# A four-stage transformer kernel on one core: another order of work at its beginning, between its stages and at its end

## The chip, the cores and the metric

The kernel runs on one core of a Trainium2 chip. A core has several engines that run side by side, each through its own queue in order: PE (TensorE) multiplies matrices and transposes, DVE (VectorE) and ACT (ScalarE) work on tiles element by element, POOL (GpSimd) also does so (a product of 128 x 512 takes it 1.26 us here, DVE 0.69) and issues the indirect DMAs, and SP (SyncE) issues the other DMAs. PE writes its products to PSUM, a small memory kept here in banks of 128 x 512 fp32 numbers; DVE, ACT and POOL bring them to SBUF. The engines wait for each other with semaphores. The metric is the device time of one execution in microseconds (us); the median of three runs is given with the lowest and the highest.

## What is computed

Sixteen sequences x of 256 tokens and 256 features, in fp32, go through four stages, each of which adds its gated result to x:

```python
x = x + tanh(g_xattn[0]) * L0_xattn(ctx, layernorm(x))   # stage 0
x = x + tanh(g_ffn[0])   * L0_ffn(layernorm(x))          # stage 1
x = x + tanh(g_xattn[1]) * L1_xattn(layernorm(x), ctx, ctx, fside, mask)   # stage 2
x = x + tanh(g_ffn[1])   * L1_ffn(layernorm(x))          # stage 3
```

- Stage 0 is attention with 16 heads of 64. The 256 queries of a sequence come from the layernorm of its normed rows; keys and values come from those rows and from 77 context rows, so 333 keys in all.
- Stage 1 is a mixture of 8 experts, each a 256 x 256 product; each token takes the two with the highest router probability. Out of the layernorm, `out = sum over the two of (x W_e + prob_e) * weight_e`.
- Stage 2 is attention with 16 heads of 16 over the 77 context rows, with a key mask; the softmax is multiplied by `fside` before the values.
- Stage 3 is gated linear attention with 8 heads of 64 in chunks of 64 tokens. A dense and a routed path are added (the routed one goes to the most probable of 4 experts for each token); then

```python
o = o * rsqrt(mean(o * o, axis=-1) + eps) * norm_w   # over the 64 values of a head
o = o * (g * sigmoid(g))
return o.reshape(B, L, 512) @ Wo
```

A layernorm is `(x - mean) / sqrt(var + 1e-5)` over the 256 features.

## The kernel before

All of x stays in SBUF: `xs[b]` holds sequence b as 128 partitions x 2 x 256. The four stages run one after the other, `stage0_fast` to `stage3_fast`, with parts of each woven into the one before. Beside the result the kernel gathers ten check values (`check`, among them `esum`, the sums of exponentials of stage 0, and `logs`, the logarithms of stage 3's mean squares). `verdict` reduces them to one flag, `bad`; SP loads it, and only if it is set does an exact, slower program run after. It does not run in the profiled execution.

Nearly all operations are put out through `dve`, `act`, `pool` and `pe` (`Pinned`), which keep each engine's instructions in the order in which the program is written. All of these carry line L50 in the profile, so the tile names tell them apart; the products and transposes of stage 3 carry L1523 and L1526. A call of a product is two instructions in the profile, since it is fp32. So the order of the work is written out by hand, by the order of the calls.

**Norms.** `moments` takes mean and variance on DVE (`bn_stats`, then `bn_aggr`, tile `mv`), then POOL adds eps and raises to the power -0.5 (tile `rs`, two small operations). `normed` lets DVE make the bias and ACT scale x, in two halves. Stage 0 norms x (`norm_x`, `normed_y`) and then the normed rows again (`norm_y`, `normed_all`), and the context rows (`norm_c`). `Prepare` (`prep`) does it for stage 2: `stats`, `norm`, `turn` (transposes, an ACT copy) and `queries`.

**Stage 0** loops over 64 units (sequence b, four heads g). `turn` makes kvT, the transposed normed rows, `all_values` the values `v`, `heads` queries and keys of two heads (PSUM to SBUF by ACT and DVE, tile `qk`), `scores` the 24 matmul instructions `sc` in three groups and three exponentials `e` on ACT. `sums` adds the three key chunks on POOL into `es`, and adds those to `esum`. `values` multiplies: `den` by ones with `es`, then e with v (48 instructions, in chunks), and DVE takes the reciprocal and the product `oT`. `project` multiplies by the output weights. A unit's values run one unit behind its scores. `heads` of the next unit is called behind the values. Stage 1's routing is called from tables (`ahead_of`, `behind_scores`, `behind_values`): its weighted rows `xw` are scattered by POOL's indirect DMAs into `rows`, sorted by expert. Before the loop stand the calls for batch 0, then the norms of batch 1, then `heads(0, 0, 0)` and `heads(0, 0, 1)`.

**Stage 1** has 48 units in two halves of 24 (eight sequences each): the rows of one expert (`xin`, fetched by SP at L1051) are transposed (`xT`, copied by ACT), multiplied (`ex`), copied by DVE (`y`) and stored by SP (L1076, `rows_out`). In the second half POOL gathers results back into x by indirect DMA (`next_gather`, 64 in all), and a table, `steps`, calls stage 2's `prep.stats` for b = 0, 1, 2.

**Stage 2** loops over b = 0 to 16; b does the scores of sequence b in two halves c (`sc`, one PSUM buffer of four banks, then one exponential of 77 x 2048 on ACT), weighs them by `fside` on DVE (`pg`), multiplies by the values, and projects sequence b-1. `prep` runs two and three sequences ahead: `prep.stats(b + 3)` stands at the end of the loop's body. In the last rounds `early` calls `next` on stage 3's generator, whose first groups (norm of sequence 0, transposes, gates, routing) so run between stage 2's parts; a letter says at which b.

**Stage 3** then loops over p = 0 to 66 for 64 positions (sequence b, pair of heads m): `keys_queries` (kq), `decays` (gq, gz), `second`, `factors` (f, q), `products` (sc), `masked` (tile `at`: DVE multiplies the dense half by a mask and, for the routed half, by `kden` and a mask; POOL adds the two), and one position later `values` (o). Every second position, `squares`, `gated` (u) and `scaled` (mean square `ms`, Ln and Exp on ACT, and POOL's product `oT`), and for each sequence `project` (16 matmul instructions, one addition on DVE, one DMA of 256 KB, L1813). PSUM tiles of its own pool `psu` have one bank each (kq, gq, gz, o). The last three rounds do only what is left of position 63, and `verdict` (L1907) stands ahead of the last `project`.

Of the kernel before, what the change touches and what calls it, by code (L numbers as in the profile page):

```python
# [17 lines left out]
P = 128  # L18
B, S, D = 16, 256, 256
S2 = 77  # L20
EPS = 1e-5
# [52 lines left out]
def layers(ctx: ExitStack, tc: tile.TileContext, t, out, check):  # L74
# [79 lines left out]
    nc.gpsimd.memset(ones, 1.0)  # L154
    gate = const("gate", [P, 4])
# [26 lines left out]
    def moments(src, p=P, n=2):  # L182
# [5 lines left out]
        for i in range(n):  # L188
            dve.bn_aggr(mv[:p, i, :], bst[:p, i, :])
        pool.tensor_scalar(rs[:p, 0, :n], mv[:p, :n, 1], 1.0, EPS, ALU.mult, ALU.add)  # L190
# [336 lines left out]
    def stage0_fast():  # L527
        with ExitStack() as sx:
# [106 lines left out]
            def values(b, g, e, es):  # L635
# [6 lines left out]
                for h, r in heads:  # L642
                    n, j = divmod(h, 2)
                    pe.matmul(den[r, :S], ones[:KC, :32], es[:, n, j * S:(j + 1) * S], start=True, stop=True)
# [39 lines left out]

            norm_c(0)
            norm_x(0)
            normed_y(0)
            norm_y(0)
            normed_all(0)
            turn(0)  # L690
            all_values(0)
            norm_c(1)
# [3 lines left out]
            heads(0, 0, 0)  # L696
            heads(0, 0, 1)
# [34 lines left out]
            values(*behind)  # L732
# [402 lines left out]
    class Prepare:  # L1135
# [12 lines left out]
        def stats(self, b):  # L1148
            self.mv[b] = moments(xs[b])
# [29 lines left out]
    def stage2_fast(prep, bank, begin):  # L1179
        with ExitStack() as sx:  # L1180
# [71 lines left out]
            for b in range(B + 1):  # L1252
# [22 lines left out]
                run(project, b - 1)  # L1275
                route.next_gather()
# [3 lines left out]
                early(a=1, b=1, c=1, d=1)  # L1280
# [224 lines left out]
    def stage3_fast(early_bank):  # L1505

        with ExitStack() as sx:
# [22 lines left out]
            eps = w1.tile([P, 1], F32, tag="eps", name="eps")  # L1530
            pool3.memset(eps, EPS)
# [219 lines left out]
            def masked(p, n):  # L1751
# [43 lines left out]
            def scaled(b, mp):  # L1795
                ps = bank("ms")
                matmul(ps, halves, sq.pop((b, mp)), start=True, stop=True)
                r = w2.tile([P, 512], F32, tag="r", name="r")
# [3 lines left out]
                pool3.tensor_tensor(oT[b][:, 2 * mp:2 * mp + 2, :].rearrange("p m s -> p (m s)"),  # L1802
                                        u_[b][:, 2 * mp:2 * mp + 2, :].rearrange("p m s -> p (m s)"), r, ALU.mult)

            def project(b):
# [7 lines left out]
                nc.sync.dma_start(out=out[b].rearrange("(c p) d -> p c d", p=P), in_=xs[b])  # L1813

# [183 lines left out]
```

## Time and profile before

| what | value |
|---|---|
| median of 3 runs | 1952.68 us (1947.13, 1952.68, 1958.38) |
| the profiled execution's own time | 1950.77 us |
| its span, first to last instruction | 1949.0 us |
| mean granted PE clock | 0.992 of full |
| busy | PE 1901.1, DVE 1088.5, POOL 1001.3, ACT 869.4 us |
| stage 0 to 1 / 1 to 2 / 2 to 3 in the span | about 980 / 1104 / 1289 us |

The page gives busy time, a row of digits per engine (40 slices of the span, in tenths), the granted PE clock in the same slices, DMA, and the groups of instructions. Behind it stands the trace, which can be asked for waits (an engine, the tile it was to write, and what ended the idle time before), for a timeline (start, duration, engine, tile written and tiles read, how many instructions are put together; in brackets the idle time before it and what ended that), and for windows (length, busy time and number of instructions of PE, PEld, DVE, ACT and POOL, then the granted clock, the DMA share and GB/s). PEld is PE's loading of weights, which runs beside its products. Starts are us from the beginning of the span.

### The profile page before, as it was taken

Reading aid. Unit: us, or ns where it says so; the run is one execution under the profiler, and the core shown is the slowest. Engines: PE = TensorE matmul, PEld = TensorE weight load, DVE = VectorE, ACT = ScalarE, POOL = GpSimd, SP = SyncE. Lnnn points to the kernel's source line nnn. Section 1 sums busy time; section 2 is a strip of 40 time slices with the busy share of each in tenths; the row PEclk is TensorE's granted clock in tenths of the full one; section 3 lists DMA queues with packets and bytes.
Section 4 is the critical chain, followed back from the end, with each engine's and each line's share of the span. In section 5 each row is a group of like instructions: output and inputs, shape, how many; then the busy total and the mean of one; then the engine's idle time right before and its main releaser. Section 6 shows DMA issues by size and latency. Waiting matters only on the chain. (4 is left out here: it accounts for less than half of the span.)

```text
span 1949.0 us, 34915 instructions
## 1 busy us (share of the span) xinstructions
PE 1901.1 (98%) x13986; PEld 1321.0 (68%) x13986; DVE 1088.5 (56%) x2635; ACT 869.4 (45%) x1795; POOL 1001.3 (51%) x905
## 2 busy tenths in 40 slices
PE   7999999999999999999999899999999999999997
PEld 4666676666766666666677666567777777777775
DVE  3334555455545545553464388875666656666564
ACT  3433344434434344343333488744444444444442
POOL 4644757556665557565614756124444444444443
PEclk9999999999999999999999999999999999999998
DMA  9300000000000000000078733000000000000000
GB/s 343 129 1 3 14 11 14 11 9 11 14 11 11 9 11 12 9 12 9 14 250 236 191 49 47 8 1 6 7 6 7 12 7 6 7 6 12 6 7 13
DMA packets 54012, 75.03 MB, mean 38 GB/s; under 512 B 10081, under 2 KB 43729, under 8 KB 53329
## 3 DMA queue, kind: packets, MB, share of 16 engines
q1 hardware_dynamic: 41552, 55.92, 8.5%
q0 software_dynamic: 12288, 16.79, 4.3%
q8 instruction: 112, 1.84, 0.4%
q14 instruction: 60, 0.48, 0.1%
HBM read 39.14 MB, written 33.55 MB: 37 GB/s over the span
## 5 line engine op out<-in xcount | busy, mean ns | idle before, releaser
L50 POOL TENSOR_SCALAR rs<-mv 128x2 f32<-128x2 f32 (+1 forms) x96 | 18.4, 192 | 468.3 <-DVE mv L50 464.4
L50 ACT ACTIVATE qk<-qk 128x256 f32<-128x256 f32 x128 | 49.2, 385 | 339.7 <-PE qk L50 339.7
L50 ACT ACTIVATE e<-sc 111x1024 f32<-111x1024 f32 x192 | 182.3, 1022 | 17.7 <-PE sc L50 17.7
L50 PE MATMUL sc<-qk 64*111 64x256 f32 x1536 | 182.2, 383 | 2.1 <-DVE qk L50 2.1
L50 PE MATMUL o<-e,v 111*32 111x256 f32 x3072 | 179.2, 382 | 0.0
L50 DVE RECIPROCAL rd<-o 128x256 f32<-128x256 f32 x64 | 112.3, 1755 | 103.0 <-PE o L50 103.0
L50 PE MATMUL v<-wkv,kvT 128*111 128x512 f32 x384 | 169.2, 597 | 0.6 <-DVE kvT L50 0.6
L50 PEld LDWEIGHTS sc<-qk 64*111 64x111 f32 x1536 | 132.1, 172 | 55.1 <-issue 28.5
L50 POOL TENSOR_TENSOR esum<-esum,es 111x512 f32<-111x512 f32 x128 | 163.1, 1274 | 10.0
L50 POOL TENSOR_TENSOR es<-e 111x1024 f32<-111x1024 f32 x64 | 151.3, 2364 | 26.5 <-ACT e L50 25.2
L50 PE MATMUL qk<-kvT,wkv 128*128 128x333 f32 x512 | 164.3, 443 | 0.0
L50 POOL TENSOR_TENSOR k<-e,ee 128x256 f32<-128x256 f32 x64 | 47.4, 740 | 222.6 <-ACT e L50 222.6
L50 POOL TENSOR_TENSOR es<-es,e 111x1024 f32<-111x1024 f32 x64 | 150.4, 2349 | 5.0
L50 PEld LDWEIGHTS o<-e,v 111*32 111x32 f32 x3072 | 100.5, 111 | 66.9 <-issue 1.7
L50 DVE COPY qk<-qk 128x333 f32<-128x333 f32 x128 | 64.5, 505 | 126.3 <-ACT qk L50 124.8
L50 PE MATMUL qk<-kvT,wq 128*128 128x256 f32 x512 | 134.3, 385 | 0.0
L50 PEld LDWEIGHTS v<-wkv,kvT 128*111 128x111 f32 x384 | 67.1, 178 | 91.6 <-issue 90.1
L50 POOL TENSOR_TENSOR at<-at,at 128x768 f32<-128x768 f32 x64 | 115.9, 1810 | 25.1 <-DVE at L50 16.0
L50 DVE TENSOR_TENSOR at<-sc,amask 128x768 f32<-128x768 f32 x64 | 61.3, 958 | 116.2 <-PE sc L1523 100.4
L50 POOL DMA_INDIRECT x<-rows_out,pos x64 | 100.4, 1568 | 35.0 <-DMA we<-in_we_dram 16.4
L50 PEld LDWEIGHTS qk<-kvT,wkv 128*128 128x128 f32 x512 | 97.2, 190 | 30.0
L50 PEld LDWEIGHTS qk<-kvT,wq 128*128 128x128 f32 x512 | 94.3, 189 | 34.0 <-issue 13.2
(230 smaller groups left out, 4125.3 us busy)
## 6 DMA issues: line engine op xcount, KB each, us to landing
rows<-zero SPq DMA_DIRECT2D x16, 640.0 KB
xin<-rows SPq DMA_DIRECT2D x16, 640.0 KB
rows_out<-y SPq DMA_DIRECT2D x16, 384.0 KB
x<-in_x_dram SPq DMA_DIRECT2D x16, 256.0 KB
rows_out<-y SPq DMA_DIRECT2D x16, 256.0 KB
out_dram<-x SPq DMA_DIRECT2D x16, 256.0 KB
wkv<-in_wkv_dram SPq DMA_DIRECT2D x2, 1024.0 KB
ew<-in_ew_dram SPq DMA_DIRECT2D x2, 1024.0 KB
```

Of the source, the lines that this page charges most:

```text
L50: x = getattr(self.engine, name)(*a, **k)
```

## The change

1. **Norms by ScalarE.** The constant `eps` is made at the program's start, on POOL, and no more at stage 3's. `moments(by_act=True)` takes Ln(var + eps) and Exp(-0.5 ...) on ACT for the two operations on POOL. It is so for the second norm of batch 0 in stage 0 and for `prep.stats` of b < 5 (three in stage 1, and those at b = 0 and 1 of stage 2).
2. **Beginning.** Products of `ones` with rows of x (four) and with the normed rows (three), into a bank that is not read, stand before the first transposes; `heads(0, 0, 0)` and `heads(0, 0, 1)` stand before the norms of batch 1.
3. **Stage 0 to 1.** In the last `values`, `den` is made from e in three chunks (12 calls for 4) and not from POOL's `es`; `es` and `esum` are still made.
4. **Stage 2 to 3.** The generator's group (norm, turn) is two groups; at b = 14 one `next` more stands after `project(13)`, and that at the end of the body at b = 16 is gone. The last three groups and the opening of `psu` become one step, which begins with `keys_queries(0)` (before, that followed them all).
5. **End.** The loop ends at p = 63. Position 63's dense and routed parts are not added on POOL; `values` multiplies them one after the other into one bank. The last `project` is in four parts (token half i, heads' half h) in the banks of kq and gq, the first ones before the last heads are there; the last scaling is on DVE, two products of `ones` into an unread bank stand beside it, and the output goes by two DMAs of 128 KB. The checks' reductions stand in three parts between these, and the flag is made after the last projection.

```diff
     nc.gpsimd.memset(ones, 1.0)
+    eps = const("eps", [P, 1])
+    nc.gpsimd.memset(eps, EPS)
     gate = const("gate", [P, 4])
...
-    def moments(src, p=P, n=2):
+    def moments(src, p=P, n=2, by_act=False):
         mv = st.tile([P, 2, 2], F32, tag="mv", name="mv")
...
             dve.bn_aggr(mv[:p, i, :], bst[:p, i, :])
+        if by_act:
+            act.activation(rs[:p, 0, :n], mv[:p, :n, 1], AF.Ln, bias=eps[:p])
+            act.activation(rs[:p, 0, :n], rs[:p, 0, :n], AF.Exp, scale=-0.5)
+            return mv, rs
         pool.tensor_scalar(rs[:p, 0, :n], mv[:p, :n, 1], 1.0, EPS, ALU.mult, ALU.add)
...
         return mv, rs
...
-            def values(b, g, e, es):
+            def values(b, g, e, es, last=False):
...
                 heads = [(h, slice(32 * h, 32 * h + 32)) for h in range(4)]
-                for h, r in heads:
-                    n, j = divmod(h, 2)
-                    pe.matmul(den[r, :S], ones[:KC, :32], es[:, n, j * S:(j + 1) * S], start=True, stop=True)
+                for c in range(3 if last else 1):
+                    for h, r in heads:
+                        n, j = divmod(h, 2)
+                        x = e[:, 3 * n + c, j, :] if last else es[:, n, j * S:(j + 1) * S]
+                        pe.matmul(den[r, :S], ones[:KC, :32], x, start=c == 0, stop=not last or c == 2)
                 for i in range(2):
...
                         for h, r in heads:
...
+            def warm(src, n):
+                ps = bank("warm")
+                for _ in range(n):
+                    pe.matmul(ps[:, :D], ones, src, start=True, stop=True)
             norm_c(0)
             norm_x(0)
+            warm(xs[0][:, 0, :], 4)
             normed_y(0)
-            norm_y(0)
+            mvs[0, "y"] = moments(y[0], by_act=True)
+            warm(y[0][:, 1, :], 3)
             normed_all(0)
...
             all_values(0)
+            heads(0, 0, 0)
+            heads(0, 0, 1)
             norm_c(1)
...
             units = [(b, g) for b in range(B) for g in range(4)]
-            heads(0, 0, 0)
-            heads(0, 0, 1)
             behind = None
...
                 ahead = units[n + 1] if n + 1 < len(units) else None
...
             run(behind_scores, B, 0)
-            values(*behind)
+            values(*behind, last=True)
             tally()
...
             run(behind_scores, B, 1)
...
         def stats(self, b):
-            self.mv[b] = moments(xs[b])
+            self.mv[b] = moments(xs[b], by_act=b < 5)
...
                 run(project, b - 1)
+                early(b=1)
                 route.next_gather()
...
                 run(prep.stats, b + 3)
-                early(a=1, b=1, c=1, d=1)
+                early(a=1, b=1, c=1)
                 route.next_gather()
...
             nc.sync.dma_start(out=halves, in_=t["halves"])
-            eps = w1.tile([P, 1], F32, tag="eps", name="eps")
-            pool3.memset(eps, EPS)
...
                                                            am[b][:, lo:hi], ALU.mult, ALU.mult)
+                    if p == last - 1:
+                        at[p] = a
+                        return
                     pool3.tensor_tensor(at[p], at[p], a, ALU.add)
-            def values(p):
+            def values(p, first=True, end=True):
                 b, m, cols = place(p)
...
                     o[b, m // 2] = psu.tile([P, 512], F32, tag="o", name="o")
-                ps, a = o[b, m // 2], at.pop(p)
+                ps, a = o[b, m // 2], at[p] if not end else at.pop(p)
                 base = m % 2 * S
...
                         matmul(ps[64 * j:64 * j + 64, to:base + S], v[b][:, i, h], a[:, j, lo:hi],
-                                         start=i == 0, stop=i == 1)
+                                         start=first and i == 0, stop=end and i == 1)
...
-            def scaled(b, mp):
+            def scaled(b, mp, by=pool3, beside=()):
                 ps = bank("ms")
                 matmul(ps, halves, sq.pop((b, mp)), start=True, stop=True)
+                for x in beside:
+                    x()
                 r = w2.tile([P, 512], F32, tag="r", name="r")
...
                 act3.activation(r, r, AF.Exp, scale=-0.5)
-                pool3.tensor_tensor(oT[b][:, 2 * mp:2 * mp + 2, :].rearrange("p m s -> p (m s)"),
+                by.tensor_tensor(oT[b][:, 2 * mp:2 * mp + 2, :].rearrange("p m s -> p (m s)"),
                                         u_[b][:, 2 * mp:2 * mp + 2, :].rearrange("p m s -> p (m s)"), r, ALU.mult)
             def project(b):
...
+            pp = {}
+            def project_part(b, i, h):
+                if h == 0:
+                    pp[i] = psu.tile([P, 512], F32, tag=("kq", "gq")[i], name=("kq", "gq")[i])
+                for m in (2 * h, 2 * h + 1):
+                    matmul(pp[i][:, :D], oT[b][:, m, tokens(i)], wo[:, m, :], start=m == 0, stop=m == 3)
+                if h == 1:
+                    dve3.scalar_tensor_tensor(xs[b][:, i, :], pp[i][:, :D], gate[:, 3:4], xs[b][:, i, :],
+                                              ALU.mult, ALU.add)
+                    nc.sync.dma_start(out=out[b, tokens(i)], in_=xs[b][:, i, :])
+            def warm():
+                ps = bank("warm")
+                for _ in range(2):
+                    matmul(ps, ones, v[B - 1][:, 0, :], start=True, stop=True)
             start = {0: [(turn, 1)], 2: [(turn_hot, 1)]}
...
             yield
-            for group in (((bias, 0), (stats, 0)), ((norm, 0), (turn, 0)), ((lows, 0),), ((gates, 0, 0),),
+            for group in (((bias, 0), (stats, 0)), ((norm, 0),), ((turn, 0),), ((lows, 0),), ((gates, 0, 0),),
                           ((gate_logs, 0, 0), (route_logits, 0)), ((route_sums, 0), (gates, 0, 1)),
-                          ((route, 0), (vals, 0), (gate_logs, 0, 1), (bias, 1)),
-                          ((turn_hot, 0), (turned_hot, 0), (stats, 1)), ((pairs, 0), (norm, 1)),
-                          ((steepest, 0, 0), (steepest, 0, 1))):
+                          ((route, 0), (vals, 0), (gate_logs, 0, 1), (bias, 1))):
                 for f, *a in group:
...
             psu = sx.enter_context(tc.tile_pool(name="f3psu", bufs=1, space=PSUM, side="right", reuse_waits="tile"))
+            keys_queries(0)
+            for f, *a in ((turn_hot, 0), (turned_hot, 0), (stats, 1), (pairs, 0), (norm, 1), (steepest, 0, 0),
+                          (steepest, 0, 1)):
+                f(*a)
             yield
...
             last = 4 * B
-            keys_queries(0)
             decays(0)
...
             dve3.tensor_scalar(wo, wo3, vec[:, V_NW:V_NW + 1], None, ALU.mult)
-            for p in range(last + 3):
+            for p in range(last):
                 run(start, p)
-                if p < last:
-                    shares(p)
-                if 0 < p <= last:
+                shares(p)
+                if 0 < p:
                     masked(p - 1, 1)
...
-                if p == last + 1:
-                    verdict(bank("verdict"))
-    def verdict(ps):
-        r = st.tile([P, 10], F32, tag="vr", name="vr")
-        bounds = (("esum", E_MOST), ("rsum", R_MOST), ("most", E_MOST), ("uneven", 0.5), ("second", E_MOST),
-                  ("logs", E_MOST), ("gates", G_MOST),
-                  ("rows", ROWS + 0.5), ("rsum2", R_MOST), ("rsum0", R_MOST))
-        for n, (name, bound) in enumerate(bounds):
-            dve.tensor_reduce(r[:, n:n + 1], check[name], AX.XY if name == "rows" else AX.X, ALU.max)
-            dve.tensor_scalar(r[:, n:n + 1], r[:, n:n + 1], bound, None, ALU.is_lt)
-        dve.tensor_reduce(r[:, 0:1], r, AX.X, ALU.min)
-        dve.tensor_scalar(r[:, 0:1], r[:, 0:1], 0.0, None, ALU.is_equal)
-        nc.tensor.matmul(ps[0:1, 0:1], r[:, 0:1], ones[:, 0:1], start=True, stop=True)
-        dve.tensor_copy(check["bad"], ps[0:1, 0:1])
+            b, p = B - 1, last - 1
+            values(p, end=False)
+            masked(p, 1)
+            project_part(b, 0, 0)
+            values(p, first=False)
+            ends = Verdict()
+            ends.part("esum", "most", "uneven", "second", "rows")
+            squares(b, 1)
+            gated(b, 1)
+            ends.part("rsum", "gates", "rsum2", "rsum0")
+            scaled(b, 1, dve3, [lambda: project_part(b, 1, 0), warm])
+            for i in range(2):
+                project_part(b, i, 1)
+            ends.part("logs")
+            ends.end(bank("verdict"))
+    class Verdict:
+        bounds = {"esum": E_MOST, "rsum": R_MOST, "most": E_MOST, "uneven": 0.5, "second": E_MOST, "logs": E_MOST,
+                  "gates": G_MOST, "rows": ROWS + 0.5, "rsum2": R_MOST, "rsum0": R_MOST}
+        def __init__(self):
+            self.r, self.n = st.tile([P, 10], F32, tag="vr", name="vr"), 0
+        def part(self, *names):
+            for name in names:
+                r = self.r[:, self.n:self.n + 1]
+                dve.tensor_reduce(r, check[name], AX.XY if name == "rows" else AX.X, ALU.max)
+                dve.tensor_scalar(r, r, self.bounds[name], None, ALU.is_lt)
+                self.n += 1
+        def end(self, ps):
+            r = self.r
+            assert self.n == len(self.bounds)
+            dve.tensor_reduce(r[:, 0:1], r, AX.X, ALU.min)
+            dve.tensor_scalar(r[:, 0:1], r[:, 0:1], 0.0, None, ALU.is_equal)
+            pe.matmul(ps[0:1, 0:1], r[:, 0:1], ones[:, 0:1], start=True, stop=True)
+            dve.tensor_copy(check["bad"], ps[0:1, 0:1])
...
         with tc.tile_pool(name="ctx_side", bufs=1) as keep, tc.tile_pool(name="f12w2", bufs=2) as keep2:
...
             stage2_fast(prep, shared_bank, last_stage)
-            for _ in range(3):
-                next(last_stage)
+            next(last_stage)
         s_banks.close()
...
             pass
```

More of the change, by code (lines that the diff above doesn't have):

```diff
@@ L1856, in stage3_fast @@
             dve3.tensor_scalar(wo, wo3, vec[:, V_NW:V_NW + 1], None, ALU.mult)
-            for p in range(last + 3):
+            for p in range(last):
                 run(start, p)
-                if p < last:
-                    shares(p)
-                if 0 < p <= last:
+                shares(p)
+                if 0 < p:
                     masked(p - 1, 1)
                 run(copies, p)
-                if 1 < p <= last + 1 and p % 2 == 1:
+                if 1 < p and p % 2 == 1:
                     gated((p - 2) // 4, (p - 2) % 4 // 2)
-                if p < last:
-                    shares_end(p)
+                shares_end(p)
                 if p + 1 < last:
@@ L1874, in stage3_fast @@
                 run(late, p)
-                if p < last:
-                    products(p, 0)
-                    masked(p, 0)
+                products(p, 0)
+                masked(p, 0)
                 run(behind_mask, p)
@@ L1885, in stage3_fast @@
                 run(logs, p)
-                if p < last:
-                    products(p, 1)
-                if 0 < p <= last:
+                products(p, 1)
+                if 0 < p:
                     values(p - 1)
```

## The prediction

> **What bounds the kernel now.** I read the page's busy times first, then the PE and clock digits, the chain of waits of PE, and the timeline at the places that it names.
>
> ```profile
> PE 1901.1 (98%) x13986; PEld 1321.0 (68%) x13986; DVE 1088.5 (56%) x2635; ACT 869.4 (45%) x1795; POOL 1001.3 (51%) x905
> PE   7999999999999999999999899999999999999997
> PEclk9999999999999999999999999999999999999998
> ```
>
> PE works 98% of the span, so time is won only where PE stands, or runs at half clock. The waits of PE, longest first (us in total, times, longest):
>
> ```profile
> PE tr L50 <- ACT xn L50: 10.8, 1, 10.8
> PE ex L50 <- ACT xT L50: 5.0, 4, 2.3
> PE o L50 <- POOL es L50: 3.2, 1, 3.2
> PE o L1523 <- POOL at L50: 3.0, 1, 3.0
> PE verdict L1907 <- DVE vr L50: 3.0, 1, 3.0
> PE tr L1526 <- DVE xn L50: 2.4, 1, 2.4
> ```
>
> They lie at the beginning, at the passages and at the end, where the change is. What a wait costs beyond itself is in the timeline and the windows:
>
> ```profile
> 13.33 12.20 PE L50 MATMUL v<-wkv,kvT 128*111 128x512 f32 x24 [0.64 <-DVE kvT L50]
> 968.09 0.64 PE L50 MATMUL o<-es,ones 111*32 111x256 f32 x8 [3.19 <-POOL es L50]
> 968.55 4.46 PE L50 MATMUL o<-e,v 111*32 111x256 f32 x48
> 13.33:16.70 3.37, 3.37 (x4) 1.37 (x5) 0.93 (x3) 0.00 (x0) 0.00 (x0) 1.00 1.09 351
> 16.70:20.10 3.40, 3.40 (x9) 1.41 (x8) 0.69 (x1) 0.59 (x1) 0.00 (x0) 1.00 1.10 348
> 969.00:972.40 3.40, 3.40 (x40) 1.72 (x36) 0.00 (x0) 0.00 (x0) 2.65 (x3) 0.50 0.00 0
> 1929.03 1.55 PE L1523 MATMUL o<-at,v 128*64 128x256 f32 x8 [3.02 <-POOL at L50]
> 1936.43 6.36 PE L1523 MATMUL proj<-wo,oT 128*128 128x256 f32 x16
> 1942.83 0.75 DVE L50 SCALAR_TENSOR_TENSOR x<-proj,gate,x 128x512 f32<-128x512 f32 x1 [6.14 <-PE proj L1523]
> ```
>
> After the 3.19 us gap the granted clock is 0.50 (the column before the last two) for one stretch of 3.4 us: 48 products take 4.46 us, against 2.77 one unit earlier. The 2.29 us gap at 991.7 and the 1.92 at 1110.8 are followed by 0.5 too. At the start four instructions of `v` run in the first 3.37 us and nine in the next 3.40: half rate, though the clock column reads 1.00. The last projection takes 6.36 us cold; warm, at 1912.96, 3.62.
>
> **The sum**, against the profiled execution's 1950.77 us (span 1949.0); the median of the runs shown is 1952.68 (1947.13 to 1958.38), 1.91 higher.
>
> *Beginning, +1.0 (-2.0 to +2.65).* POOL's two steps (0.19 and 0.69 us) with their hand-overs, 8.85 to 9.85, become two small ACT operations of some 0.2 (rows with 128x2 elements on ACT are 0.17 to 0.21): 0.5 saved. The 14 added matmul instructions go into PE's first 10.76 us, idle now, so they cost nothing; if they came late, the transposes would queue behind them, 14 x 0.2 at most. They may raise the clock before `v`. Its first 3.4 us at half rate lose 1.7, and the transposes lose 0.45. With the 0.5 that is 2.65. Against it: with heads(0,0) moved past the norms of batch 1, DVE's statistics for c and x, POOL's powers and ACT's y(1), hidden before under the head products, come after the copies of qk. The exps stand in ACT's order behind y(1) (1.09): 34.45 less the gain, where they began at 32.81, and sc(0,1) comes at 39.75 less the gain, where it was at 38.59: 1.15 lost, 1.5 left. PE then stands 1.3 and 2.35 in 5.5 us, and such gaps halve the clock for a stretch (1.7) in some places and not in others: half of it is 0.85. I take 1.0, between 1.5 and 0.65. The lower end is without warm products (2.15 less) and with the whole stretch (0.85 less). The eps memset (0.69 on POOL at 1107.94, for which nobody waits) goes to POOL's idle start: nothing; before the first rs it has 2.09 us of cover, and beyond that would delay the start by 0.69.
>
> *Stage 0 to 1, +4.0 (+2.3 to +4.0).* den reads e directly: 24 instructions for 8, 16 x 2.77/48 = 0.92 more. e is there since 962.34, so the 3.19 goes, and the half clock behind it (4.46-2.77 = 1.7): 3.19+1.7-0.92 = 4.0. POOL's es and esum stay, for the checks, beside PE. Next late is xin's transfer: on SP it waits for PE's values and for POOL's esum (968.12+2.63 = 970.75), so its issue moves from 973.20 to 970.9 only, 2.3 earlier. Had it only just landed at 980.03, where xT reads it without a wait, the gain would be 2.3. But three loads of 640 KB are under way until 981.6, and xT needs the first: I take 4.0. The scatters that POOL issues next wait for landings as before and stand ahead of no product.
>
> *Stage 1's second half, +1.7 (0 to +2.1).* POOL full of gathers (1.54 each) gives rs at 1078.3 for statistics that were done at 1070.54, and ex waits 2.14 at 1080.18 for ACT's xT behind xn. By ACT, rs is there at 1071. Each Ln holds ACT for DVE's statistics: 0.45 over the three places, in which ACT's xT copies are queued and PE waits for them.
>
> *Stage 2, b=0 and 1, -3.0 (0 to -6.0).* No wait is taken away here, and one is added. ACT's Ln stands before the next exp and waits for bn_aggr: at 1118.2 where the exp started at 1116.94 (delay 1.7), and 1130.25 where it started at 1128.07:
>
> ```profile
> 1127.94 0.66 PE L50 MATMUL tr<-ident,xn 128*128 128x128 f32 x4
> 1128.07 1.96 ACT L50 ACTIVATE e<-sc,neg 77x2048 f32<-77x2048 f32 x1
> 1129.91 0.30 DVE L50 BATCH_NORM_AGGREGATE mv<-bst 128x2 f32<-128x6 f32 x2
> ```
>
> With two ops of 0.2 the second exp is 2.6 late. The sc at 1130.39 has one PSUM buffer and needs that exp's end (1130.03, then 1132.6): PE stands 2.2. At b=0 the sc at 1120.35 needs 1118.9+1.7 = 1120.6: 0.25. Behind the waiting Ln stand the exp, gpx's and xnT's copies; DVE's pg and PE's q wait for those. 2.45 in all, and 0.55 for the chance (a third) that the gap halves the clock. Both delays in full (4.3) and a whole stretch (1.7) make 6.0; if the later waits of this stage absorb them, 0. POOL, relieved of two powers here, had slack.
>
> *Stage 2 to 3, +1.0 (+0.3 to +1.7).* project(13), ready at 1254.66, now fills the 2.45 us in which turn(0) waits for xn at 1256.26: +1.73. keys_queries(0) ahead of turn_hot(0) puts eight matmul instructions (1.13 and 1.03 overlapping, 1.84) before hT; hT's copy then no longer stands 0.39 behind the addition on DVE, so DVE's chain (em, am, xn, steepest, f) is 1.45 later: f ended at 1288.18, now 1289.63, and kq(1), which has one bank and came at 1288.91, waits for it: -0.74. If the chain is not later, +1.7; if it is later by all of 1.45, +0.3.
>
> *End, +8.2 (+7.6 to +8.7).* values(63) no longer waits for POOL's add (1927.17, 1.80): its two halves, with project's first part between, end at 1928.5 instead of 1930.58. sq .60, ms warm 1.12 and Ln, accumulator, Exp .69+.19+.63 bring r at 1931.7 (before 1934.9); DVE multiplies in .69 instead of POOL's 1.26; eight matmul instructions remain, 1.8 warm, and an addition of .43: 1934.98 instead of 1943.58, 8.6 earlier. Two warm products (four instructions of .5) lie in the 1.5 us wait for r, behind project's part; if they ran cold, 4 us, they would delay the last part. The two stores of 128 KB need one more SP issue (.37), the first 0.9 early. The checks' reduces (.68 for esum, .41 for rsum, the rest .15 to .2) stand between on DVE and are done before r. The verdict, finished ahead of the projection before, now ends behind it: the last reduces, product and copy come some 1.2 after the addition. The span ended 5.4 after the addition; with bad later it is 5.4 to 6.4. Hence 8.2, half-way; the ends add the half us either side.
>
> Sum: 1.0+4.0+1.7-3.0+1.0+8.2 = 12.9, so 1937.9 against its own time and 1939.8 against the median; I take **1939**.
>
> The Trainium skill, "TensorE: Matmul & The Clock Gate", section "HAM oscillation", has the rule of no idle gaps above about 3.4 us. By it the gap of 3.19 would cost no clock, stage 0 to 1 would bring 1.7 less and the sum would be 11.2. The row with 0.50 after that gap speaks against it. Its section "What's actually happening" calls the window free-running, which speaks against the products ahead: they might be undone by its phase, 2.15 less in the sum.
>
> **Rivals.** *Hidden waits:* stage 2 absorbs both delays and the start gains in full: 12.9+3.0+1.65 = 17.5, 1935. The spare buffer of e speaks for it, the single sc bank against. *Only the end:* beginning and passages give their 4.7 back to what is late next (xin, ACT's order, f): 8.2, 1944.5. For it: 5.0 us of waits for xT in four places show stage 1 bound by ACT's chain. *Not as it says:* the products ahead raise no clock; `v` keeps 12.20: 12.9-2.15 = 10.75, 1942. *Slower:* in stage 2 the stalls at b=0 and 1 start half-clock stretches that feed on themselves, as ACT is busy 9.1 of 10.03 us in each b and regains little. A stretch of 3.41 costs 1.7; it takes 12.9/1.7 = 8 of them to no gain, and 14 to 0.5% slower, 48 us. Against it: the half clock from 1112.4 ended by itself at 1119.2.
>
> **Numbers.** Chances: forecast .50 (own range 1934 to 1944), hidden .13, only the end .24, no warm-up .07, slower .06. 0.5% is 9.8 us, about what this measurement can tell: the bound is 1942.9. Above it in gain lie .40 of the forecast's, all .13, .06 and .03: .62 faster. .06 slower, .32 same. The bounds of the terms, added, give gains of 2.2 to 19.2; with the runs' own spread the range is 1930 to 1949.
>
> **What would show it.** `v` x24 in 10.3 and starting near 12.4; sc(0,1) before 38.5; no wait for es near 965, no 0.50 after it; xT copies without 2.14; a stall of sc on e of some 2.2 in the second b of stage 2; tr at the passage without a wait; the last projection in parts without a 6 us row, last store issued 8 us earlier. The prediction is wrong if stage 2's stall repeats, xin is waited for, or the tail grows beyond 6.4 us.

## The result, and the profile after

The changed kernel takes 1944.62 us (median of 13 runs, 1939.97 to 1950.34), the kernel before 1952.10 in as many runs beside it (1947.13 to 1960.44): a ratio of 0.9952, with a 95% interval of 0.9937 to 0.9967. By the medians that is 7.5 us less (0.38%); the ratio goes by the means, 1944.36 against 1953.72, which is 9.4 us (0.48%). It is faster beyond doubt, and by either figure inside the 0.5% that the prediction drew as the bound of "same". The profiled execution took 1940.42 us with a span of 1938.6: it is one of the fastest of the 13, 4.2 below their median, while the profile before lies 1.3 below its own. So profile against profile the gain is 10.35 us, and the terms below add up to that.

The page of the changed kernel, the lines that answer to those shown before:

```profile
PE 1902.5 (98%) x14028; PEld 1322.9 (68%) x14028; DVE 1089.7 (56%) x2637; ACT 871.8 (45%) x1807; POOL 992.4 (51%) x891
PE   8999999999999999999999899999999999999997
PEclk9999999999999999999999999999999999999999
```

Its list of waits of PE (us in total, times, longest):

```profile
PE sc L50 <- ACT e L50: 4.3, 4, 2.3
PE warm L50 <- DMA x<-in_x_dram: 3.7, 1, 3.7
PE ex L50 <- ACT xT L50: 3.6, 4, 2.3
PE o L50 <- DVE pg L50: 2.0, 1, 2.0
PE sc L50 <- DVE qk L50: 1.8, 1, 1.8
```

The waits for es, for POOL's last at, for xn at the passage to stage 3 are gone from the top. At the head now stands one that the list before had at 0.6: sc waits for ACT's exp. What is not on this list is the time after PE's last product, and there lay the largest miss.

The place of the same instruction in both timelines tells where the time went. The marks are the starts of the reciprocal behind unit 62 of stage 0 (963.99 before, 962.50 after), the first copy of xT (980.73, 975.16), the first exp of stage 2 (1105.64, 1095.77), its exp number 30 (1252.04, 1247.17), the Ln of the last mean square but one (1922.24, 1915.93) and the end of the span.

| stretch | predicted gain | gain in the profiles |
|---|---|---|
| beginning and stage 0 | +1.0 | +1.49 |
| stage 0 to 1 | +4.0 | +4.08 |
| stage 1, to the first exp of stage 2 | +1.7 | +4.30 |
| stage 2, first rounds | -3.0 | -5.00 |
| passage to stage 3, and stage 3 up to its last but one mean square | +1.0 | +1.44 |
| end | +8.2 | +4.04 |
| sum | 12.9 | 10.35 |

The timeline after, at the places that the prediction named:

```profile
12.65 10.55 PE L50 MATMUL v<-wkv,kvT 128*111 128x512 f32 x24 [0.64 <-DVE kvT L50]
963.35 1.50 PE L50 MATMUL o<-e,ones 111*32 111x256 f32 x24
964.67 2.77 PE L50 MATMUL o<-e,v 111*32 111x256 f32 x48
1111.45 1.10 PE L50 MATMUL sc<-qT,kd 32*77 32x256 f32 x16 [1.45 <-ACT e L50]
1121.01 0.30 DVE L50 BATCH_NORM_AGGREGATE mv<-bst 128x2 f32<-128x6 f32 x2
1121.35 0.30 ACT L50 ACTIVATE rs<-mv,eps 128x2 f32<-128x2 f32 x1 [2.29 <-DVE mv L50]
1121.78 1.95 ACT L50 ACTIVATE e<-sc,neg 77x2048 f32<-77x2048 f32 x1
1123.88 1.50 PE L50 MATMUL sc<-qT,kd 32*77 32x256 f32 x16 [2.32 <-ACT e L50]
1928.40 0.48 DVE L50 SCALAR_TENSOR_TENSOR x<-gq,gate,x 128x256 f32<-128x256 f32 x1 [0.38 <-PE gq L1542]
```

`v` runs warm from its first product; the wait for es and the slow 48 products are gone; in stage 2 ACT stands idle for 2.29 us at the Ln, and behind it the exp and then PE's sc are late. The last addition ends at 1928.88 where it ended at 1943.58, 14.7 earlier, and yet the span ends only 10.4 earlier.

### The profile page after: what moved, and what is told of

It reads as the page before. It is cut to its first block, busy times and chain, and to the rows that moved or that the text cites. A ratio compares the mean times of both kernels' runs of the same rounds, so it can differ in the third digit from the quotient of the medians.

```text
span 1938.6 us, 34988 instructions
## 1 busy us (share of the span) xinstructions
PE 1902.5 (98%) x14028; PEld 1322.9 (68%) x14028; DVE 1089.7 (56%) x2637; ACT 871.8 (45%) x1807; POOL 992.4 (51%) x891
## 3 DMA queue, kind: packets, MB, share of 16 engines
q8 instruction: 112, 1.84, 0.4%
## 4 chain that ended last, share of the span: by engine, by line
PE 93%; DVE 2%; ACT 1%; DMA 1%; SPq 1%; issue 0%; POOL 0%; ACTq 0%; POOLq 0%; DVEq 0%
PE o L50 13%; PE qk L50 13%; PE sc L50 10%; PE v L50 9%; PE proj L50 7%; PE kq L1542 6%; PE sc L1542 5%; PE ex L50 3%; PE gq L1542 3%; PE v L1542 3%; PE proj L1542 3%; PE o L1542 3%; PE gz L1542 2%; PE z L1542 2%; PE den L1542 1%; PE q L50 1%
## 5 line engine op out<-in xcount | busy, mean ns | idle before, releaser
L50 POOL TENSOR_TENSOR es<-e 111x1024 f32<-111x1024 f32 x64 | 151.3, 2365 | 25.1 <-ACT e L50 23.9
```

What stands on the lines that cost most here:

```text
L50: x = getattr(self.engine, name)(*a, **k)
```

## The experiments

Each kernel starts from the changed one ("after") or from the one before, as said. The half-clock time named below is that of the granted-clock records between 20 and 1900 us of the span.

**1. The flag early (from after).** The flag's last reduction stands behind the last Ln, its product ahead of the projection's last parts.

```diff
-            scaled(b, 1, dve3, [lambda: project_part(b, 1, 0), warm])
+            scaled(b, 1, dve3, [lambda: project_part(b, 1, 0), warm], lambda: (ends.part("logs"), ends.least()))
+            ends.end(bank("verdict"))
             for i in range(2):
                 project_part(b, i, 1)
-            ends.part("logs")
-            ends.end(bank("verdict"))
```

> The changed kernel, with the flag's last reduction, product and copy ahead of the last two parts of the projection instead of behind them. Theory T (the part of the end that was not gained lies behind the flag: every engine loads it, branches past the slow program, and POOL then drains for 2.81 us; before the change ACT, POOL and PE did this beside the last projection): the copy of the flag comes about 3.3 us earlier against the last addition, POOL's branch and drain lie beside the projection's parts, and the time from the last addition (1928.88 in the changed kernel) to the end of the span falls from 9.7 to between 5.4 and 6.6 us; the kernel gains 3 to 4 us. Rival R (the tail is set by the two stores landing, or by SP): the time from the last addition to the end stays at 9 to 10 us, and nothing is gained.

Measured: from the last addition's end (1930.13) to the span's end (1935.9) 5.8 us, in place of 9.7; median 1942.07 (1937.8 to 1945.99), ratio to before 0.9944 (0.992 to 0.9968). What POOL does with the flag, from the view of the line that branches on it (duration min/median/max in ns, first and last start in us); before:

```profile
L68 POOLq TENSOR_LOAD <-bad x1: 495/495/495, 1936.7 to 1936.7; - x1
L68 POOLq EVENT_SEMAPHORE  x1: 17/17/17, 1940.3 to 1940.3; - x1
L68 SPq TENSOR_LOAD <-bad x1: 486/486/486, 1944.0 to 1944.0; - x1
```

after:

```profile
L68 POOLq TENSOR_LOAD <-bad x1: 496/496/496, 1930.1 to 1930.1; - x1
L68 PEldq COMPARE_BRANCH  x1: 3647/3647/3647, 1930.7 to 1930.7; - x1
L68 POOLq EVENT_SEMAPHORE  x1: 17/17/17, 1934.9 to 1934.9; - x1
```

and, after again, the view of the program's last line:

```profile
L2054 POOLq DRAIN  x3: 46/107/2810, 1935.0 to 1938.3; - x3
L2054 POOLq EVENT_SEMAPHORE  x4: 17/17/17, 1937.8 to 1938.5; - x4
```

and with the flag early:

```profile
L68 POOLq TENSOR_LOAD <-bad x1: 490/490/490, 1927.9 to 1927.9; - x1
L68 POOLq EVENT_SEMAPHORE  x1: 17/17/17, 1931.3 to 1931.3; - x1
L68 SPq TENSOR_LOAD <-bad x1: 513/513/513, 1930.6 to 1930.6; - x1
```

Once the flag is there every engine loads it (0.5 us) and branches past the slow program. POOL's next instruction comes 2.8 to 4.2 us after its branch, and then a drain of 2.81 us (DRAIN in the view), on which the last semaphores wait. Before, POOL did this from 1936.7, beside the projection, and had it done at 1943.2. In the changed kernel all of it lies behind the flag, 8.6 us from 1930.07 to the end. Early, the load and the branch lie beside the projection's last parts, and the drain (1931.4 to 1934.2) beside SP's last waits: theory T holds, its rival falls. From the Ln of the last mean square but one to the end of the span the four changed kernels with the flag early (1, 8, 9 and 11) take 19.0 to 19.6 us, the six others 22.3 to 22.7. The medians alone could not tell: the ratio is 0.9944 here and 0.9952 for the changed kernel.

**2. Stage 2's statistics by POOL (from after).**

```diff
-            self.mv[b] = moments(xs[b], by_act=b < 5)
+            self.mv[b] = moments(xs[b], by_act=b < 3)
```

> The changed kernel with the two statistics in stage 2 (b = 3 and 4 of x) by POOL again, the three in stage 1 by ACT. Theory T (Ln on ACT waits for DVE's statistics, in order ahead of the next exp, and sc has one PSUM buffer): the waits of sc for e in the first two rounds of stage 2 (1.45 and 2.32 us) go, and with them the half-clock stretch behind the second; stage 2 takes 4 to 5 us less. Rival R (these rounds wait for something else as soon as the exps come earlier, such as DVE's pg or the gathers): less than 1.5 us of the 5 come back, and another wait of PE of 1 to 2 us shows in the same two rounds.

Measured: from the first exp of stage 2 to exp 30 the kernel gains 0.34 us on the one before, where after loses 5.00: 5.3 back. Its waits of PE have sc for e at 0.6 us in two waits, as before the change, and no longer at the head:

```profile
PE ex L50 <- ACT xT L50: 3.6, 4, 2.3
PE warm L50 <- DMA x<-in_x_dram: 3.4, 1, 3.4
PE o L50 <- DVE pg L50: 2.1, 2, 1.7
PE sc L50 <- DVE qk L50: 1.8, 1, 1.8
PE k L50 <- DVE vc L50: 1.5, 1, 1.5
```

Median 1936.63 (1935.59 to 1937.83, four runs), ratio 0.9904 (0.9879 to 0.993): 8.0 us below after's median, from other runs, of which the trace shows 5.3 at this place. T holds. Not all of the 5.3 is the stalls: after has one half-clock stretch more between these marks (10.2 us for 6.8). Profiles with 6.8 us of it take 146.1 to 147.4 us here with the statistics by POOL (before, 2, 4, 7, 11) and 150.2 to 150.5 with them by ACT (1, 5, 6, 12), so the two stalls by themselves cost about 4.

**3. The last denominators alone (from before).** `values(*behind, last=True)` with its three-chunk `den`, nothing else.

> The kernel before, with only the last denominators of stage 0 made from e in three chunks. Theory T: the wait for es (3.19) and the half clock behind it go, at 0.9 of added products: stage 1's first transposes come 4.0 to 4.1 us earlier against the unit before, as in the changed kernel, without any other part of the change. Rival R (part of that gain belongs to other parts, or xin's transfer is late next): 2.3 to 3.2 us, with a wait of xT for xin.

Measured: between the same two marks it gains 4.08 us, as after does, and xT starts without a wait. The term stands by itself: all eleven profiles with this `den` have 12.66 us between the marks, where before has 16.74. The execution as a whole was only 1.2 us shorter than the profile before: 17.1 us of half clock against 13.7, most of it in the first rounds of stage 2.

**4. The wait filled (from before).**

```diff
+            ps = bank("warm")
+            for _ in range(6):
+                pe.matmul(ps[:, :D], ones, xs[0][:, 0, :], start=True, stop=True)
             values(*behind)
```

> The kernel before, with 12 matmul instructions of 128x256 into an unread bank put into the wait for es between stage 0 and 1 (about 2.4 of its 3.19 us). The wait itself stays. Theory T (the gap itself lowers the granted clock of the stretch behind it): no stretch of 0.50 follows, the 48 products take 2.77 us and not 4.46, and stage 1 begins about 1.7 us earlier. Rival R (the lower clock has another cause, or needs idle time beyond 3.4 us as the skill's page has it): the 48 products take 4.46 as before and nothing is gained.

In this kernel's timeline and windows (length, busy time and count of PE, PEld, DVE, ACT, POOL, then clock, DMA share, GB/s):

```profile
965.05 2.84 PE L50 MATMUL warm<-x,ones 128*128 128x256 f32 x12
968.39 0.64 PE L50 MATMUL o<-es,ones 111*32 111x256 f32 x8 [0.50 <-POOL es L50]
968.84 2.77 PE L50 MATMUL o<-e,v 111*32 111x256 f32 x48
979.65 1.09 PE L50 MATMUL xT<-ident,xin 128*128 128x128 f32 x8 [0.84 <-DVE x L50]
969.00:972.40 3.40, 3.40 (x56) 2.08 (x45) 0.72 (x1) 0.00 (x0) 2.95 (x3) 1.00 0.00 0
```

The values begin as late as before, and the clock stays at 1.00: 2.77 us for the 48 products instead of 4.46. Kernel 7, which has the same wait unfilled (3.2 us), shows half clock behind it as well, from 966.7 to 973.5. So it was the idle time that cost the clock, and 3.19 us were enough. The rule in the Trainium skill, "TensorE: Matmul & The Clock Gate", section "HAM oscillation", to have no idle gaps of PE above some 3.4 us, draws the line too high for this case: a gap of 3.19 was enough here. The second half of T fell: of the 1.7 us, 0.84 went into a new wait of xT, and with other small shifts stage 1 began 0.62 earlier. The trace puts that wait down to DVE's addition; but before the change xT started ahead of the same addition, so the cause is another, and xin, whose issue came at 971.81, is the likeliest; that was not tried.

**5. The norms of batch 1 first (from after).**

```diff
-            all_values(0)
+            all_values(0, lambda: (norm_c(1), norm_x(1)), lambda: normed_y(1))
             heads(0, 0, 0)
             heads(0, 0, 1)
-            norm_c(1)
-            norm_x(1)
-            normed_y(1)
```

> The changed kernel with the norms of batch 1 (statistics of c and x, and ACT's y) woven between the copies of v of batch 0, ahead of heads(0,0), instead of behind them. Theory T (in the changed kernel the exps of the first scores stand on ACT behind y(1), which is late because its statistics come behind the copies of qk; that costs PE 0.87 and 1.84 us): the first exp starts about 1.2 us after its scores' start and not 4.9, both waits of PE go, and the reciprocal of unit 2 comes 2.0 to 2.7 us earlier against the first product of v. Rival R (x of batch 1 lands too late, or the next norm takes its place): v's copies wait for DVE's statistics, and less than 1 us is won.

Measured: the first exp starts 1.17 us after its scores (4.85 in after), and the two waits of 0.87 and 1.84 are gone. Against the first product of `v` the reciprocal of unit 2 came only 1.19 earlier (60.41 us behind it, 61.60 in after), short of the 2.0 to 2.7 expected, but `v` took 12.42 us here in place of 10.55. With that 1.87 taken off it is 3.1: the two waits (2.7) and a little.

**6. Without the products ahead (from after).** The two calls of `warm` are left out.

> The changed kernel without the seven products (14 matmul instructions) ahead of the first transposes. Theory T (they raise the granted clock before v): v's 24 instructions take 11.5 to 12.3 us in place of 10.55, at half rate for their first 2 to 3.4 us, and the reciprocal of unit 2 comes 1.5 to 2.2 us later against x's landing. Rival R (the clock rises at a time that has nothing to do with PE's work, or the products only push the transposes): v takes 10.6 as in the changed kernel.

Measured: `v` takes 13.01 us, and the reciprocal comes 2.43 later, both more than expected (11.5 to 12.3, and 1.5 to 2.2). In the five profiles without these products (before, 3, 4, this one and 7) `v` takes 12.20 to 13.16; in the eight with the change's own it takes 10.55 six times, and 12.30 and 12.42 in the other two. The granted-clock records agree: the first one, at full clock, begins at 16.7 to 18.7 us in the five (what lies ahead of it has no record, which the windows show as 1.00), at 7.6 to 12.0 in the six, and at 16.3 and 16.7 in the two. So they do raise the clock, but not every time: the same products, at almost the same times in the span, were enough in one execution and not in another.

**7. Stage 1's statistics alone by ACT (from before).** `by_act=b < 3` in `prep.stats`, and eps at the start.

> The kernel before, with only the three statistics of stage 1's second half by ACT. Theory T (the 2.14 us wait for xT came from rs behind POOL's gathers): from y of unit 24 to the last y, 1.0 to 1.5 us less than before; nothing changes elsewhere in stage 1, so that the rest of the 4.3 us which the changed kernel gained in stage 1 was the half-clock stretch behind the 2.29 us gap at 991.7 and the masks' transfers. Rival R (all 4.3 belong to the statistics): 4 us less over stage 1.

Measured: from y of unit 24 to the last y it takes 44.77 us, 1.08 less than before, and the wait of 2.14 is 0.71. Outside of that nothing was won in stage 1. That is not yet what the edit is worth. All profiles with the statistics by ACT have 44.77 us here, but with POOL it was 45.85 before, 45.41 in kernel 3 and 44.41 in kernel 4, where the wait is 0.71 as well: the wait depends on where POOL's gathers lie in the execution, and the edit brings between -0.4 and +1.1.

Nor is the rest of after's 4.30 the change's. The wait of 2.29 at its place is followed by half clock in the profile before and not in the profile after (1.7), and between y of units 5 and 24 another 1.56 was won, where two short waits of PE for DVE (at 1021.8 and 1038.1 before) are gone. Kernel 4, whose stage 1 is that of before, wins the same without the change: it has 120.2 us from the first copy of xT to the first exp of stage 2, after 120.6, before 124.9; and other profiles of changed kernels have up to 127.8.

**8. Three edits together (from after): 1, 2 and 5.**

> The changed kernel with three edits together: the flag early, the two statistics of stage 2 by POOL, the norms of batch 1 between v's copies. Theory T: the terms add: 3.6 + 5 + 2 to 2.7, about 11 us below the changed kernel, 1932 to 1935 us median, 0.9% below the kernel before or more. Rival R (the gains overlap, since half-clock stretches and late transfers come with other phases): 5 us or less below the changed kernel.

Measured: 1934.15 us (1929.39 to 1936.84), ratio to before 0.9896 (0.9868 to 0.9924). It is 10.5 below the median of after, though from other runs. It beats both kernels, and T holds: the median is within the 1932 to 1935 that its sum gave. In its profile a wait for xT early in stage 1 had grown from 2.29 to 4.58 us, with 6.8 us of half clock behind it. POOL's `rs`, for which ACT's norm ahead of the copy of xT waits, came 2.4 us after its statistics were done there, behind a scatter and memsets:

```profile
979.49 0.30 DVE L50 BATCH_NORM_AGGREGATE mv<-bst 128x2 f32<-128x6 f32 x2
982.17 0.19 POOL L50 TENSOR_SCALAR rs<-mv 128x2 f32<-128x2 f32 x1
```

**9 and 10. The routing's statistics of the last sequence by ACT, in that version and alone (from after).**

```diff
-            self.mv[b] = moments(xs[b])
+            self.mv[b] = moments(xs[b], by_act=b == B - 1)
```

> The version with the three edits together (flag early, stage 2's statistics by POOL, norms of batch 1 between v's copies), and the routing's statistics of the last sequence by ACT. Theory T (what stands between the expected sum of the three edits and the measured one is the wait for xT early in stage 1, 4.58 us there and 2.29 in the changed kernel, since rs is on POOL behind a scatter that waits for landings and three memsets): that wait falls to 1 us or less, with the half-clock stretch behind it; the median is 3 to 6 us below the version without it (1934.15), 1928 to 1931. Rival R (ACT then waits for something else at that place, or the next wait takes it over): the wait stays above 2 us and the median within 2 us of 1934.15.

> The changed kernel with only the routing's statistics of the last sequence by ACT. Theory T: the wait for xT near 986 (2.29 us in the changed kernel) falls below 1 us, and the tenth expert's y comes 1.5 to 2.3 us earlier against the first xT. Rival R: it stays above 2 us.

Measured: the wait is 2.81 us with the other edits (4.58 without this one) and 2.40 alone (2.29 in after). With the other edits 1.8 us came back, for POOL was late there; in the changed kernel it was not (its `rs` starts 0.1 us behind the statistics), and nothing came back. Neither wait falls below 1 us, so the theory falls. The timeline of the second says why:

```profile
982.91 0.30 DVE L50 BATCH_NORM_AGGREGATE mv<-bst 128x2 f32<-128x6 f32 x2
983.24 0.30 ACT L50 ACTIVATE rs<-mv,eps 128x2 f32<-128x2 f32 x1 [4.34 <-DVE mv L50]
983.68 0.57 ACT L50 COPY xT<-xT 128x512 f32<-128x512 f32 x1
984.30 3.33 PE L50 MATMUL ex<-ew,xT 128*128 128x256 f32 x8 [2.40 <-issue]
```

ACT waits 4.34 us for the statistics, which stand on DVE behind the routing's small operations, and the copy of xT queues behind the Ln, as the exp did in stage 2. The medians, 1931.81 (1929.13 to 1934.81) and ratio 0.9894 (0.9878 to 0.9911) for the first, can't be told from version 8's.

**11. A longer run of products at the beginning, in version 9.** Eight products of ones by ones (16 instructions) before x lands, two calls in place of four on x.

> The same version with 16 short products of ones by ones at the beginning, before x has landed, and two calls in place of four on x. Theory T (whether the products ahead raise the clock in time depends on where their start lies in the clock's windows, so that a longer run of them does it always): v's 24 instructions take 10.5 to 10.6 us, the transposes are not later than 10.2 to 10.9, and the median is 0 to 1.5 us below the same version without them. Rival R (they queue ahead of the transposes): the first transpose starts after 11.0 us and the median is higher.

Measured: `v` took 12.25 us. Theory and rival both fell: the transposes were early (10.26), the clock was up by then (its first record begins at 5.6), and it went down again from 12.4 to 15.8, after gaps of 1.32 and 0.60 us. Median 1933.68 (1931.06 to 1935.68), ratio 0.9896 (0.988 to 0.9913): nothing won.

**12. keys_queries(0) at the end of the passage again (from after).**

> The changed kernel with keys_queries(0) again at the end of the passage to stage 3, behind the pairs and the norm, as before the change. Theory T (its place ahead of turn_hot makes DVE's chain late, and kq(1) waits 0.91 us for f): the wait of kq for f goes, the wait for hT is 1.0 instead of 0.6, and am of sequence 2 comes 0.3 to 0.9 us earlier against the last exp of stage 2. Rival R (the place ahead hides as much as it costs): less than 0.3 us either way.

Measured: the wait of kq for f is gone and that for hT is 1.04, as T has it. But two half-clock stretches lay in this passage (1265.5 to 1268.9 and 1282.6 to 1286.0), and from exp 30 to am of sequence 2 the passage takes 1.6 us more than before, where after takes 1.1 less. Its net worth stays open.

## Why the prediction was right, and where it was not

The median lies 5.6 us above the 1939 forecast and within the range, and the side was right; the size, 7.5 for 13, fell just on the "same" side of the bound, which had .32. Two large terms fell short, and a third came out larger by luck, which hid part of them. By one of its own signs the prediction was wrong at the end: the tail grew beyond 6.4 us.

- *End.* The working to the last addition held: 8.4 us earlier with the shift of 6.3 taken off, where 8.6 was worked out. The step that failed is the tail, "5.4 to 6.4 now": it measured 9.7. I asked how late bad's load by SP would be, and did not ask what the other engines did with the flag in the 6 us before. POOL's way out (branch and 2.81 us of drain) had been covered by the projection; the change took the cover off. Experiment 1 shows it, and puts 3.6 us of it back.
- *Stage 2.* The place and the mechanism were right (ACT in order, one buffer of sc), the size was not: 5.0 for 3.0. The second stall was 2.32 (2.2 worked out), the first 1.45 and not 0.25. The 0.25 was read off the profile before, where PE ran at half clock ahead of this place (1112.4 to 1119.2) and came to it late; in after it ran at full clock from 1107.4 on and came sooner, from one sc to the next in 4.40 us of work where before took 5.48. The half clock, put at a third of a stretch, came in full: behind the second stall sc and q took 4.50 us, 2.86 before. Experiment 2 gives 5.3 back; of it about 4 are the price of the stalls, the rest is that stretch.
- *Stage 1.* The mechanism was there, but it is not steady: the edit brings between -0.4 and +1.1 (experiment 7) against the 1.7 forecast. The 4.30 is luck, since kernel 4 wins it without the edit; what made stage 1 faster in these two profiles, beyond the 1.7 of clock, stays open.
- *Stage 0 to 1.* Right, 4.08 for 4.0, for the reasons given, but the bound at 2.3 was not one: the first xin went out at 967.64, before esum's end (969.31). Only PE's end had to come first.
- *Beginning.* 1.49 for 1.0. sc(0,1) came at 37.10, as worked out (39.75 less 2.65), and the lost 1.15 was there as waits of 0.87 and 1.84; the half clock that I put behind them did not come, so the gain was the 1.5 that the prediction had without it. Experiment 6 confirms that the products ahead raise the clock; that they may fail, which I priced at 2.15, happened in two profiles of eight. That the phase of the clock's stretches decides it is likely, not shown.
- *Passage.* +1.44 for +1.0. From exp 30 to the next it is 9.90 us for 11.62, the 1.73 that project(13) was to bring; kq(1) waits 0.91 for f as foretold (0.74), and from there to the last mark 0.28 is lost.
- Of the rivals, "hidden waits" fell with stage 2. "Only the end" had the nearest figure (1944.5), but not its mechanism: the passages did gain. "Slower" has its mechanism in part: half clock in the first rounds of stage 2 did last up to 17 us in one profile, but it ended.

What moves the medians beside these terms is half clock. Two of the profiles differ only in one pair of small operations (after, and experiment 10): 10.2 and 23.9 us of half clock, 13.7 more, of which half is 6.8; the spans are 1938.6 and 1945.2. The profile after was lucky in this, and so the median's gain is 7.5 and not 10.4: its mean granted clock was 0.996, the median of the 13 runs' is 0.994, and 0.002 of the span is 3.9 us, about the 4.2 that it lies below their median.

## What to carry to other kernels

Ask of every operation that is moved to an in-order engine what stands behind it there, and of its input when it is ready: in stage 2 the small Ln cost about 4 us more than the POOL operations that it replaced, and alone in experiment 10 it won nothing. When a change shortens the last stretch, list what every engine still does until the end of the span, since work that the stretch covered does not shrink with it. And where one execution is profiled, take half-clock stretches off before a difference is given a cause.

## What was unexpected of the hardware

- A half-clock stretch does not end just because PE is busy. In experiment 10 it lasted from 1104.3 to 1121.3, five stretches, with PE busy throughout but for the first 0.2 us, as these windows show (clock is the column before the last two):

```profile
1107.70:1111.10 3.40, 3.40 (x29) 1.29 (x22) 1.29 (x4) 0.89 (x3) 2.93 (x2) 0.50 0.53 77
1111.10:1114.50 3.40, 3.40 (x28) 1.81 (x32) 1.27 (x5) 2.06 (x3) 3.10 (x4) 0.50 0.56 75
1118.00:1121.30 3.30, 3.30 (x9) 2.58 (x9) 2.77 (x4) 1.76 (x2) 0.00 (x0) 0.50 0.17 25
1121.30:1124.70 3.40, 3.40 (x41) 2.21 (x39) 1.53 (x2) 1.81 (x4) 0.00 (x0) 0.99 0.00 0
```

  Most of what ran until 1117.57 were products over 32 rows or 32 columns (tiles 32*77 and 77*32); then came eight of 128*128, and the clock rose one stretch later. That the small products don't count in full is a reading of this, not tried by itself; against it, in the profile before the rounds of stage 2 from 1119.2 on run the same products at full clock.
- The same wait has different prices: 2.29 us without a product were followed by half clock in the profile before and not in the profile after. Stretches start on a grid of 3.413 us: in the profile before at 969.01, 992.90, 1112.37 and 1928.15, which are 7, 35 and 239 steps apart. The grid lies elsewhere in each execution.
- With nothing to cover it, leaving the changed kernel takes 8.6 us from the end of the flag's copy to the end of the span, 2.81 of them in one drain of POOL.
